# A chunk-attention and nearest-neighbour kernel: gather masks made from 256 columns, half of a comparison on ScalarE, a new order of the step, and a packed three-layer MLP

## The chip, the cores and the metric

The kernel runs on one core of a Trainium2 chip. The metric is the device time in microseconds (us) of one execution. The kernel before took 5687.46 us, the median of three runs (5677.63 to 5689.53).

A core has a matrix engine (PE, TensorE), whose weight loads are shown apart as PEld, and three engines for work by element: DVE (VectorE), ACT (ScalarE) and POOL (GpSimd). SP (SyncE) issues the DMAs here. Every engine takes its instructions in the order in which they were written; it waits where an operand is not there yet, and all that is queued behind waits with it.

## The reference

There are 32 batches. The input `x` and the context `ctx` are 32 x 128 x 1024. First comes attention in chunks of 64 positions with 8 heads, queries, keys and values all made from the context, then a residual and a normalisation over positions:

```
out = attention(ctx, ctx, ctx, mask) @ W_out.T + b_out + x
x1  = (out - mean(out)) * rsqrt(var(out) + 1e-5)
```

In the second part the context's 128 channels x 1024 positions are read again: for each of the 1024 positions the 30 nearest others (128-dimensional distance, 30 of 1024) are found. The second part takes the context as if it had three coordinates, that is, its first three rows serve as the coordinates of a point:

```
idx   = top_k(2 p.p' - |p|^2 - |p'|^2, 30)
rel   = pts[idx] - pts                      # three coordinates
sph   = (rho, theta, phi) of rel
feat  = concat(sph, sph - mean(sph))        # 6 features
h     = lrelu(bn(feat @ W1.T))              # 6 channels
h     = lrelu(bn(h @ W2.T))                 # 3 channels
h     = lrelu(bn(h @ W3.T))                 # 1 channel
att   = softmax(h over the 30 neighbours)
y     = x1 + sum over neighbours of x1[idx] * att
```

Each `bn` takes its mean and variance over all batches, points and neighbours, so each layer must have been computed for all 32 batches before the next one can be applied.

## The kernel before

The kernel has three stages, each with its own order of instructions fixed by `written_order`.

**Stage 1, the loop.** 256 steps, one per block of 128 points (8 blocks per batch). It is a software pipeline that is written out by hand in `step` (lines 899 to 947): in step `s` the engines work on block `s` (top-30), `s-1` (splitting the indices), `s-2` (one-hot masks and the gather), `s-3` (summing the gather) and `s-4` (relative coordinates). Work that happens once per batch (projections, values, normalisation, the features of a whole batch) is put into the steps by `plan` and issued by `do(s - 0.5)` and `do(s)`.

The parts that matter here, each with its lines:

- `eight` (639): three instructions of DVE (the 8 largest of 1024, their positions, their removal), four times per step, on `ds`, which ACT copies from PSUM one step ahead in `distances_copy` (631).
- `exponents` (499): DVE takes the maxima of the scores `sc`, ACT makes eight exponentials; `normalize` (512): a reciprocal on DVE, then a product on POOL.
- `split_indices` (648), `turn_indices` (655), `spread_indices` (663): the 30 indices of each point, padded to 32 slots, are written as hi = index / 8 and lo = index mod 8, turned by PE so that slots are rows, copied by ACT into `ht` (64 x 128) and written to DRAM (`hl`). SP then reads hi back as one row of 4096 columns for all 128 partitions (`hb`, 1 MB) and lo as 1024 columns (`lb`, four DMAs).
- `last_onehot` (686) and `onehot` (692): `hb` becomes a one-hot mask by comparing with the partition number. DVE does 3072 of the 4096 columns in one `is_equal`; ACT does the other 1024 as Abs and then Relu(1 - x). PE multiplies it with the coordinates (24 matmuls, `ps_g`), `evicted` (719) copies the product to `mk`.
- `lows` (713): the same pair of ACT instructions on `lb` makes lo's mask; `masked` (728): POOL multiplies `mk` with it; `summed` (735): eight matmuls into `ps_r`, which has one buffer; `found` (749) copies it on ACT, `relative` (754) subtracts on POOL.
- `turned`, `turned_copy`, `attend` (517 to 549): the probabilities are turned by PE, copied by ACT, multiplied with the values by PE, and copied by ACT into `ots`.
- `features` (764): a generator that is advanced 13 times per batch, every half step, by `turn`; its element work is on POOL, its functions on ACT.

The order of a step before, by engine: ACT has `last_onehot`, the exponentials, `split_indices`, `ht`, `distances_copy`, `turned_copy`, `lows`, `ots`, `found`, the half-step extras, `evicted`, the extras. PE has `distances`, `turn_indices`, `turned`, the 24 matmuls, `attend`, half-step extras, `scores`, `summed`, extras. DVE has the maxima, `eight` 0, `is_equal`, `eight` 1 and 2, the reciprocal, `eight` 3.

**Stage 2, the MLP** (lines 980 to 1129). The features of a batch were written to DRAM as 3 x 30720 values and come back as 120 partitions (3 channels x 40 groups) x 768 columns. The first pass computes layer 1 as four matmuls of 120 x 120 weights and 384 columns, and layer 2 as four more; the matrices hold the layer's weights in blocks, so that most entries are zero. The second pass applies layer 2's normalisation and computes layer 3; its result `zz` is written to DRAM (two DMAs, line 1102) and read back by point as `Z` (line 1103).

**Stage 3, the weighted sum** (lines 1132 to 1314). It is not touched by the change.

Of the kernel before, what the change touches and what calls it, by code (L numbers as in the profile page):

```python
# [9 lines left out]
F32 = mybir.dt.float32  # L10
U32 = mybir.dt.uint32
I32 = mybir.dt.int32
# [45 lines left out]
def kernel(ctx: ExitStack, tc: tile.TileContext, aps: dict, out: bass.AP):  # L58
# [57 lines left out]
    pi = const.tile([P, 4], I32, tag="pi", name="pi")  # L116
    nc.gpsimd.iota(pi[:, 0:1], pattern=[[0, 1]], base=0, channel_multiplier=1)
    nc.vector.tensor_scalar(pi[:, 1:2], pi[:, 0:1], 7, None, ALU.bitwise_and)
    nc.vector.tensor_scalar(pi[:, 2:3], pi[:, 0:1], 31, None, ALU.bitwise_and)
    pf = const.tile([P, 8], F32, tag="pf", name="pf")  # L120
    nc.vector.tensor_copy(pf[:, 0:3], pi[:, 0:3])
    pcol, lo_p = pf[:, 0:1], pf[:, 3:4]
    nc.vector.tensor_scalar(pf[:, 5:6], pf[:, 2:3], 24.0, None, ALU.is_lt)
    nc.vector.tensor_scalar_add(lo_p, pf[:, 1:2], 1.0)
    nc.vector.tensor_mul(lo_p, lo_p, pf[:, 5:6])
    nc.vector.tensor_scalar_add(lo_p, lo_p, -1.0)
    less_p = const.tile([P, 1], F32, tag="less_p", name="less_p")
    nc.vector.tensor_scalar_mul(less_p, pcol, -1.0)
    less_lo = const.tile([P, 1], F32, tag="less_lo", name="less_lo")
    nc.vector.tensor_scalar_mul(less_lo, lo_p, -1.0)  # L130

    own2 = const.tile([P, NJ, 2, 2], F16, tag="own2", name="own2")
    nc.vector.tensor_scalar(pi[:, 3:4], pi[:, 0:1], 3, None, ALU.logical_shift_right)
    nc.vector.tensor_copy(pf[:, 6:7], pi[:, 3:4])
    for j in range(NJ):
        for n, (col, base) in enumerate(((pf[:, 6:7], OFF + 16 * j), (pcol, 128 * j))):
            nc.vector.tensor_scalar_add(
                own2[:, j, n, :], col.to_broadcast([P, 2]), float(base)
            )
# [45 lines left out]
    def spread(name, n):  # L185
# [19 lines left out]

    NQ = 40
    NR = P * E // NQ
    CQ = 3 * NQ
    assert NR * NQ == P * E and NR % 2 == 0 and NR // 2 <= 512
    dd = const.tile([P, 3, NQ], F32, tag="dd", name="dd")  # L210
    nc.gpsimd.memset(dd, 0.0)
    nc.gpsimd.affine_select(
        out=dd, in_=dd, compare_op=ALU.not_equal, fill=1.0, base=0,
        pattern=[[-NQ, 3], [-1, NQ]], channel_multiplier=1,
    )
    own_c = const.tile([P, 3], F32, tag="own_c", name="own_c")
    nc.vector.tensor_reduce(own_c, dd, AX.X, ALU.add)
    own_q = const.tile([P, NQ], F32, tag="own_q", name="own_q")
    nc.vector.tensor_reduce(own_q, dd.rearrange("p c q -> p q c"), AX.X, ALU.add)

    def of_channel(pool, name, w, n, c=None):

        t = pool.tile([P, n, 3], F32, tag=f"{name}_3", name=f"{name}_3")
        if c is None:
            c = pool.tile([P, n], F32, tag=name, name=name)
        nc.vector.tensor_mul(t, w, own_c.unsqueeze(1).to_broadcast([P, n, 3]))
        nc.vector.tensor_reduce(c, t, AX.X, ALU.add)
        return c

    def matrix(name, w, n):  # L230

        m = const.tile([P, n, NQ], F32, tag=name, name=name)
        nc.vector.tensor_mul(
            m,
            own_q.unsqueeze(1).to_broadcast([P, n, NQ]),
            of_channel(const, f"{name}_w", w, n).unsqueeze(2).to_broadcast([P, n, NQ]),
        )
        return m.rearrange("p n q -> p (n q)")
# [14 lines left out]
    kv_h = const.tile([P, 2, 6], F32, tag="kv_h", name="kv_h")  # L253
    we_h = const.tile([P, 2, 3], F32, tag="we_h", name="we_h")
    for to, w, n in ((kv_h, kv, 6), (we_h, we, 3)):
        for h in range(2):
            of_channel(
                const, f"of_{n}_{h}", w[:, 3 * h : 3 * h + 3, :].rearrange("p c f -> p f c"), n,
                to[:, h, :],
            )  # L260
    bn1_h = [
        of_channel(const, f"bn1_h{i}", w.rearrange("p (h c) -> p h c", c=3), 2)
        for i, w in enumerate(bn_w[0])
    ]
    bn2_h = [of_channel(const, f"bn2_h{i}", w.unsqueeze(1), 1) for i, w in enumerate(bn_w[1])]

    mx1 = matrix("mx1", we, 6)
    w2s = const.tile([P, 2, 3, 3], F32, tag="w2s", name="w2s")
    nc.vector.tensor_copy(w2s, w2.rearrange("p (i h c) -> p h i c", h=2, c=3))
    mx2 = matrix("mx2", w2s.rearrange("p h i c -> p (h i) c"), 6)  # L270
# [4 lines left out]
        mx3[:, 0:NQ], own_q, of_channel(const, "mx3_w", w3.unsqueeze(1), 1), None, ALU.mult  # L275
    )
    avg_c = const.tile([P, 3, NQ], F32, tag="avg_c", name="avg_c")
    nc.vector.tensor_scalar_mul(
        avg_c, own_c.unsqueeze(2).to_broadcast([P, 3, NQ]), 1.0 / NQ
    )  # L280
    avg_c = avg_c.rearrange("p c q -> p (c q)")
# [9 lines left out]
    def root(pool, dst, v, shape, tag):  # L291
# [12 lines left out]
    sph_d = [dram.tile([3, P * E], F32, tag=f"sph_{b}", name=f"sph_{b}") for b in range(B)]  # L304
# [3 lines left out]
        [dram.tile([2 * SL, P], BF16, tag=f"hl_{b}_{j}", name=f"hl_{b}_{j}") for j in range(NJ)]  # L308
        for b in range(B)
# [8 lines left out]
    with ExitStack() as part:  # L318
# [11 lines left out]
        for j in range(NJ):  # L330
            w = p1.tile([P, 3, SL], F16, tag=f"wt{j}", name=f"wt{j}")
            nc.gpsimd.memset(w[:, 0, :], 0.0)

            nc.gpsimd.tensor_copy(w[:, 1:3, KNN:SL], own2[:, j])
            wts.append(w)
        for i in range(2):
# [6 lines left out]
            for name, rows in (("mb3", mb3s), ("nx3", nx3s)):  # L343
                m = p1.tile([P, T], BF16, tag=f"{name}{i}", name=f"{name}{i}")
                nc.gpsimd.memset(m, 0.0)
                rows.append(m)

# [150 lines left out]

# [842 lines left out]
```

## Time and profile before

The profiled execution took 5682.62 us by the clock of the runs; its span, from the first to the last instruction, is 5680.9 us.

| engine | busy us | share of the span |
|---|---|---|
| PE | 4305.4 | 76% |
| DVE | 5210.7 | 92% |
| ACT | 4105.8 | 72% |
| POOL | 2354.1 | 41% |

The stages can be told by what runs: the loop's last `is_equal` starts at 4212.0 us; the first matmul of the MLP starts at 4259.8, the last statistics of its first pass are made at 4431, those of its second pass at 4524; the first matmul of stage 3 starts at 4555.

A line of the list of groups names the source line, the engine, the operation, what is written and read, the shapes and the count, then the busy time in us and the mean length of one in ns, then how long the engine stood idle before such instructions and what ended most of that. The lines around the loop's rows:

```profile
L643 DVE MAX8 top<-ds 128x8 f32<-128x1024 f32 x1024 | 1250.5, 1221 | 10.3 <-ACT ds L634 4.6
L716 ACT ACTIVATE lb<-lb,less_lo 128x1024 bf16<-128x1024 bf16 x256 | 296.9, 1160 | 0.0
L689 ACT ACTIVATE hb<-hb,less_p 128x1024 bf16<-128x1024 bf16 x256 | 293.5, 1146 | 17.6 <-DMA hb<-hl 16.3
L717 ACT ACTIVATE lb<-lb 128x1024 bf16<-128x1024 bf16 x256 | 270.9, 1058 | 8.1
```

The first says that the 8 largest are taken 1024 times at 1221 ns, and that DVE hardly waits before them. The other three are ACT's comparisons, lo's (716, 717) and the quarter of hi's (689), each 1024 columns wide.

### The profile page before, as it was taken

Reading aid. Unit: us, or ns where it says so; the run is one execution under the profiler, and the core shown is the slowest. Engines: PE = TensorE matmul, PEld = TensorE weight load, DVE = VectorE, ACT = ScalarE, POOL = GpSimd, SP = SyncE. Lnnn points to the kernel's source line nnn. Section 1 sums busy time; section 2 is a strip of 40 time slices with the busy share of each in tenths; the row PEclk is TensorE's granted clock in tenths of the full one; section 3 lists DMA queues with packets and bytes.
Section 4 is the critical chain, followed back from the end, with each engine's and each line's share of the span. In section 5 each row is a group of like instructions: output and inputs, shape, how many; then the busy total and the mean of one; then the engine's idle time right before and its main releaser. Section 6 shows DMA issues by size and latency. Waiting matters only on the chain. (4 is left out here: it accounts for less than half of the span.)

```text
span 5680.9 us, 127216 instructions
## 1 busy us (share of the span) xinstructions
PE 4305.4 (76%) x48908; PEld 2593.5 (46%) x48908; DVE 5210.7 (92%) x6990; ACT 4105.8 (72%) x9798; POOL 2354.1 (41%) x2736
## 2 busy tenths in 40 slices
PE   6766776776677677767767776677749589999999
PEld 3433443443344334334433443334325167777776
DVE  8999999999999999999999999999975597888876
ACT  5777777777777777777777777777755576666665
POOL 3455555555655555555555555555540000000000
PEclk8878878787878888787888788788869699999999
DMA  2333333333233233333323333333322233333332
GB/s 84 108 107 105 121 112 109 108 111 111 102 116 115 102 111 116 113 110 111 111 103 110 115 107 111 111 105 117 109 92 69 72 84 98 96 97 97 95 98 84
DMA packets 318510, 589.60 MB, mean 104 GB/s; under 512 B 147408, under 2 KB 207568, under 8 KB 285136
## 3 DMA queue, kind: packets, MB, share of 16 engines
q1 hardware_dynamic: 317904, 581.47, 30.8%
q8 instruction: 387, 6.34, 0.5%
q14 instruction: 219, 1.79, 0.1%
HBM read 439.66 MB, written 74.45 MB: 90 GB/s over the span
## 5 line engine op out<-in xcount | busy, mean ns | idle before, releaser
L643 DVE MAX8 top<-ds 128x8 f32<-128x1024 f32 x1024 | 1250.5, 1221 | 10.3 <-ACT ds L634 4.6
L644 DVE FIND_INDEX8 idx<-top,ds 128x8 uint32<-128x1024 f32 x1024 | 1248.4, 1219 | 0.0
L646 DVE MATCH_REPLACE8 ds<-top,ds 128x1024 f32<-128x1024 f32 x768 | 928.8, 1209 | 0.0
L659 PE MATMUL ps_hl<-ident,wt 128*64 128x128 f16 x256 | 74.0, 289 | 1116.8 <-ACT wt L653 1116.0
L1293 PEld LDWEIGHTS <-oh 128*128 128x128 bf16 x24576 | 692.2, 96 | 333.7 <-issue 288.0
L506 ACT ACTIVATE pr<-sc,mx 128x64 f32<-128x64 f32 x2048 | 610.8, 323 | 207.7 <-DVE mx L502 138.5
L1293 PE MATMUL pss<-apart,oh 128*128 128x32 bf16 x24576 | 697.1, 176 | 41.8 <-DMA apart<-bc 34.7
L703 PE MATMUL ps_g<-hb,tp 128*32 128x512 bf16 x6144 | 651.9, 589 | 94.3 <-DVE hb L697 92.8
L758 POOL TENSOR_TENSOR rel<-got 128x90 f32<-128x90 f32 x256 | 108.3, 423 | 1359.1 <-ACT got L751 1358.9
L659 PEld LDWEIGHTS <-wt 128*64 128x64 f16 x256 | 30.7, 120 | 1306.7 <-ACT wt L653 1306.7
L733 POOL TENSOR_TENSOR mk<-mk,lb 128x512 f32<-128x512 f32 x512 | 623.5, 1238 | 1.8
L1224 DVE TENSOR_TENSOR oh<-h,ihi 128x4096 bf16<-128x4096 bf16 x256 | 584.6, 2284 | 18.6 <-PE pss L1293 18.2
L740 PEld LDWEIGHTS ps_r<-sel,mk 128*128 128x128 f32 x4096 | 511.6, 203 | 181.7 <-issue 79.2
L624 PE MATMUL pd<-cx 128*128 128x512 f32 x992 | 577.4, 666 | 0.0
L1245 PE MATMUL acc<-al,xtr 128*128 128x512 f32 x1024 | 565.5, 635 | 0.6 <-ACT al L1303 0.6
L740 PE MATMUL ps_r<-sel,mk 128*128 128x12 f32 x4096 | 535.8, 269 | 6.1 <-POOL mk L733 4.8
L1303 ACT COPY al<-pss 128x512 f32<-128x512 f32 x512 | 296.5, 585 | 223.5 <-PE pss L1293 220.3
L515 POOL TENSOR_TENSOR pr<-pr,sm 128x512 f32<-128x512 f32 x256 | 267.0, 1043 | 427.5 <-DVE sm L514 375.0
L506 ACT ACTIVATION_READ_ACCUMULATOR pr<-sc,mx 128x1 f32 x2048 | 442.5, 216 | 0.0
L703 PEld LDWEIGHTS <-tp 128*32 128x32 bf16 x6144 | 223.3, 130 | 405.3 <-issue 393.1
L1221 ACT COPY h<-hi 128x1024 bf16<-128x1024 bf16 x256 | 268.0, 1048 | 119.8 <-DVE oh L1224 119.5
L484 PE MATMUL sc<-kx,qT 128*64 128x512 f32 x1024 | 324.0, 714 | 10.4 <-DMA kx<-kT 7.3
(337 smaller groups left out, 8762.5 us busy)
## 6 DMA issues: line engine op xcount, KB each, us to landing
hb<-hl SPq DMA_DIRECT2D x256, 1024.0 KB
lb<-hl SPq DMA_DIRECT2D x1024, 64.0 KB
apart<-bc SPq DMA_DIRECT2D x1024, 48.0 KB
mb<-in_mask_Bx1x_ff_dram SPq DMA_DIRECT2D x32, 512.0 KB
xb<-in_x_dram SPq DMA_DIRECT2D x32, 512.0 KB
kx<-kT SPq DMA_DIRECT2D x512, 32.0 KB
x<-xb SPq DMA_DIRECT2D x32, 512.0 KB
xt<-xt SPq DMA_DIRECT2D x32, 512.0 KB
```

The lines of the kernel that those rows point to most:

```text
L484: nc.tensor.matmul(dst, qT[:, te : te + CHUNK], kx[:, :, te : te + CHUNK], start=True, stop=False,)
L506: nc.scalar.activation(pr_t[:, i, :], sc[:, i, :], AF.Exp, bias=mx[:, i : i + 1], accum_out=sm[:, i, :],)
L624: nc.tensor.matmul(pd, cx[:, j * P : (j + 1) * P], cx[:, sl], start=True, stop=False)
L643: nc.vector.max(top[:, sl], ds)
L644: nc.vector.max_index(idx[:, sl], top[:, sl], ds)
L646: nc.vector.match_replace(ds, top[:, sl], ds, GONE)
L703: nc.tensor.matmul(pg[e * 32 : (e + 1) * 32, :], tp[:, i, :], oh[:, e * 1024 + r * 512 : e * 1024 + (r + 1) * 512], start=(i == 0), stop=( ...
L733: nc.gpsimd.tensor_mul(half, half, lb[:, r * 512 : (r + 1) * 512])
L740: nc.tensor.matmul(pr.rearrange("p (e k) c -> p k e c", k=8)[:, k], mk[:, k, :], sel2, start=True, stop=True,)
L1224: nc.vector.tensor_tensor(oh.rearrange("p g a i -> p a g i"), h32.to_broadcast([P, 4, 32, 32]), ihi.to_broadcast([P, 4, 32, 32]), ALU.is_e ...
L1245: nc.tensor.matmul(acc.rearrange("p c g a -> p (c g) a"), xt[:, l, :], al[:, l], start=(l == 0), stop=(l == NJ - 1),)
L1293: nc.tensor.matmul(ps[:, k, :], oh[:, g].rearrange("p a i -> p (a i)"), bm[:, :, i, g, :], start=(i == 0), stop=(i == 2),)
```

## The change

1. **lo's mask.** `split_indices` writes hi and lo's source four times side by side (120 columns instead of 30). `turn_indices` makes, beside the old 64 x 128 product, two products of 128 x 128 in which every row is one pair (slot, value of lo); PE gets seven matmuls instead of two. ACT turns these 256 columns into the mask `lc` (Abs, Relu), SP writes it to DRAM (`lo`, 64 KB) and reads it back spread as `lb`, which is then a finished mask. `lows` is gone.
2. **hi's comparison.** DVE does 2048 columns, ACT 2048.
3. **A gate.** A POOL instruction of one element reads DVE's half of the mask before `masked`, so that POOL's products start after the comparison.
4. **The order of a step** as in the diff. The maxima come after `eight` 0; ACT's exponentials after the comparisons; `summed` before `scores` and `attend`; `found` before `summed`; `normalize` last. In `spread_indices` the read of `hb` is issued before the write of `nb`.
5. **`features`** is cut into 20 parts (`TURNS`), advanced every half step.
6. **The MLP** gets its data as four groups of 32 rows (30 used: 3 channels x 10 groups). Layer 1 is eight matmuls of 30 rows x 64 weight columns, layer 2 eight of 64 rows x 32 columns, in an order in which neighbours have other rows, columns and PSUM banks; `ps_h` gets three buffers. In the last layer `z` has five buffers instead of three, and the read of `Z` is issued two turns later than the write that it waits for (`by_point`).

```diff
         def turn_indices(s):
-            pt = ps_1.tile([2 * SL, P], F32, tag="ps1", name=f"ps_hl_{s}")
-            nc.tensor.matmul(pt, wt[:, SL : 3 * SL], ident1, start=True, stop=False)
-            nc.tensor.matmul(pt, wt[:, 0 : 2 * SL], ident8, start=False, stop=True)
+            hi4, all4 = flat[:, SL : 5 * SL], flat[:, 5 * SL : 9 * SL]
+            pt = ps_1.tile([P, 3, P], F32, tag="ps1", name=f"ps_hl_{s}")
+            once = pt[0 : 2 * SL, 2, :]
+            nc.tensor.matmul(once, flat[:, 4 * SL : 6 * SL], ident1, start=True, stop=False)
+            nc.tensor.matmul(once, flat[:, 0 : 2 * SL], ident8, start=False, stop=True)
+            for h in range(2):
+                nc.tensor.matmul(pt[:, h, :], all4, ident1, start=True, stop=False)
+                if h == 1:
+                    nc.tensor.matmul(pt[:, h, :], less4, ident1, start=False, stop=False)
+                nc.tensor.matmul(pt[:, h, :], hi4, ident8, start=False, stop=True)
         def spread_indices(s):
...
+            lc = p2.tile([P, 2, P], BF16, tag="lc", name=f"lc_{s}")
+            nc.scalar.activation(lc, pt[:, 0:2, :], AF.Abs, bias=from_lo)
+            nc.scalar.activation(lc, lc, AF.Relu, bias=1.0, scale=-1.0)
+            dl = lo_d[b][j]
+            nc.sync.dma_start(dl.rearrange("h x n -> x h n"), lc)
...
+            by_l = dl.rearrange("h (q e k) n -> (h q) e (k n)", q=4, e=4)
             for e in range(4):
                 nc.sync.dma_start(
                     lb[e * 32 : (e + 1) * 32, :],
+                    by_l[:, e, :].unsqueeze(0).to_broadcast([4, 8, 8 * P]),
                 )
         def last_onehot(s):
-            rest = near[s][0][:, 3 * 8 * P :]
+            rest = near[s][0][:, 2 * 8 * P :]
         def onehot(s):
-            first = oh[:, 0 : 3 * 8 * P]
+            first = oh[:, 0 : 2 * 8 * P]
...
-        def lows(s):
...
+        def gate(s):
+            passed = p2.tile([1, 1], BF16, tag="passed", name=f"passed_{s}")
+            nc.gpsimd.tensor_copy(passed, gates.pop(s)[0:1, 0:1])
         def step(s):
...
+            if past(1):
+                split_indices(s - 1)
             if past(2):
                 last_onehot(s - 2)
...
             if now:
                 eight(s, 0)
+            if now and s > 0:
+                maxima(s)
+                exponents(s)
             if past(1):
                 turned(s - 1)
             if 0 <= s and s + 1 < S:
                 distances_copy(s + 1)
             if past(2):
                 onehot(s - 2)
+                gate(s - 2)
+            if past(3):
+                masked(s - 3)
             if past(4):
                 found(s - 4)
                 relative(s - 4)
             if past(2):
                 evicted(s - 2)
             if past(3):
                 summed(s - 3)
+            if past(1):
+                turned_copy(s - 1)
             if now:
                 eight(s, 1)
...
             if s + 1 < S and s >= 0:
                 scores(s + 1)
+            if past(1):
+                attend(s - 1)
+            do(s - 0.5)
             if now:
                 eight(s, 2)
             do(s)
             if now:
                 eight(s, 3)
+                normalize(s)
```

```diff
+        TURNS = [(r, (r + w) % 2) for w in range(2) for r in range(4)]
         def first_layer(b):
...
+            for r, i in TURNS:
+                rows = slice(32 * r, 32 * r + 30)
+                nc.tensor.matmul(
+                    pss[r // 2][64 * (r % 2) : 64 * (r % 2) + 64, i, 0:half],
+                    mx1[rows], x[rows, i * half : (i + 1) * half], start=True, stop=True,
+                )
         def second_layer(b):
...
+            for r, i in TURNS:
+                rows = slice(64 * (r % 2), 64 * (r % 2) + 64)
+                nc.tensor.matmul(
+                    ps[32 * r : 32 * r + 32, i, 0:half],
+                    mx2[rows], hs[r // 2][rows, i * half : (i + 1) * half],
+                    start=True, stop=True,
+                )
         def third_layer(b):
...
-            z = q2.tile([P, half], F32, tag="z", name=f"zz_{b}", bufs=3)
+            z = q2.tile([P, half], F32, tag="z", name=f"zz_{b}", bufs=5)
...
+        def by_point(b):
             nc.sync.dma_start(Z[:, b, :], z_d[b].rearrange("(p e) -> p e", e=E))
```

The features are written by four DMAs per batch instead of one, and one more DMA per batch (`clear`) fills the unused rows with zeros.

## The prediction, made before the changed kernel was run

> **What bounds the kernel now.** I read the busy time by stretch first, over a piece of the loop and over the two passes of the MLP (columns: us; busy us and count of PE, PEld, DVE, ACT, POOL; granted clock; DMA share; GB/s).
>
> ```profile
> 1000.00:4000.00 3000.00, 2131.78 (x16266) 1197.29 (x16264) 2951.95 (x4112) 2318.33 (x6255) 1702.78 (x1953) 0.81 0.32 110
> ```
> ```profile
> 4259.00:4431.00 172.00, 167.89 (x514) 94.63 (x514) 93.52 (x145) 90.55 (x98) 0.00 (x0) 0.99 0.20 59
> 4437.00:4524.00 87.00, 46.27 (x128) 9.44 (x128) 46.32 (x69) 44.78 (x64) 0.00 (x0) 0.54 0.27 82
> ```
>
> DVE is busy 2952 of 3000 us in the loop: it is the bound, and the list of waits has no entry for it there. The maxima (line 502) start first at 34.9 and last at 4183.0 us, so 255 steps take 16.27 us each. The first MLP pass is PE's (168 of 172 us). In the second no engine is busy for more than 54%: something is waited for.
>
> For what ACT does in its idle 682 us I read its waits over the same 3000 us, some 184 steps or 23 batches (us, times, longest), and SP's:
>
> ```profile
> ACT qT L459 <- PE ps_q L458: 119.4, 46, 3.4
> ACT f_ay L822 <- POOL f_ay L821: 95.5, 23, 4.3
> ACT pr L506 <- DVE mx L502: 87.1, 63, 3.2
> ACT ht L667 <- PE ps_hl L660: 87.1, 184, 0.6
> ACT ots L547 <- PE ps_ot L540: 71.9, 115, 1.4
> ```
> ```profile
> SPq L669 <- ACT ht L667: 1771.8, 184, 14.9
> ```
>
> Only 87 us of it, with 51 us behind POOL before the same exponentials, is ACT waiting for the slower loop. ACT works 12.57 us per step and waits 3.70; without those 138 us and 6 us of DMA its own chain, waits on PE included, is 15.5 us per step against DVE's 16.27. **That is the thin margin on which this change turns.** SP has 9.6 us per step to spare.
>
> **DVE's part.** Its comparison shrinks from 3072 to 2048 columns.
>
> ```profile
> L697 DVE TENSOR_SCALAR hb<-hb,pf x256: 1008/1012/1871, 65.0 to 4212.0; 128x3072 bf16<-128x3072 bf16 x128
> ```
>
> Minimum, median and maximum: half of them take 1.01 us, the others are stretched while POOL runs its product with lo's mask beside them (mean 1.204). The gate keeps that product away, so I start from 1.01. A third less in proportion gives 0.67; with some 0.2 us fixed (the reciprocal of 8 columns takes 0.194) it is 0.74. I take 0.74: 1.204 - 0.74 = 0.46 us, and DVE could step in **15.81 us**. What the gate delays: POOL stands before `masked`, `relative`, the extras and the product in `normalize`, for which PE's `summed` and `turned` wait. POOL works 1703 / 184 = 9.2 us per step, so about 4 us lost between the last product and the comparison fit; in the step with `features` parts 15 and 16 and the splits POOL ends late, but PE's next gather waits for ACT's masks anyway. Without that cover 0.2 to 1 us in one step of eight.
>
> **ACT's part, per step.** ACT's length grows by (1.900 - 1.048) / 1024 = 0.83 ns per column, from the 2048-column cast of line 1195 and the 1024-column copy of line 1221.
> - hi: 1024 columns more in two instructions: +1.70.
> - `lows` gone: 1160 + 1058 ns less about 0.06 of overlap: -2.16.
> - `lc`, 256 columns: 0.364 (ht, 128 columns from PSUM) + 0.11, then 1.058 - 0.64, less overlap: +0.83.
> - the split's 90 more columns in two instructions: +0.15.
>
> Sum +0.52: 13.09 us of work. The waits count as much. PE's seven small matmuls (0.1 to 0.3 each) lie under the 3.9 us of `last_onehot` that now come before `ht`, so the 0.47 us wait for `ht` goes. But `ots` becomes late. `ps_r` has one buffer; PE may start `summed` only when ACT's `found` has emptied it, and the new order puts `scores` and `attend` behind `summed`. One step of PE before:
>
> ```profile
> 2542.93 0.40 PE L540 MATMUL ps_ot<-pts,vx 128*32 128x64 f32 x16
> 2543.27 1.08 PE L484 MATMUL sc<-kx,qT 128*64 128x512 f32 x4
> 2544.18 0.39 PE L488 MATMUL sc<-mb,ones 128*64 128x512 bf16 x2
> 2544.49 1.96 PE L740 MATMUL ps_r<-sel,mk 128*128 128x12 f32 x16
> 2546.38 1.04 PE L375 MATMUL ps_c<-ident,cx 3*128 3x3 f32 x8
> ```
>
> Start to start: attend 0.34, scores 1.22, summed 1.89; in the steps around it up to 0.58, 1.96 and 1.81. With the middle of these PE needs 1.8 + 1.5 + 0.5 + 0.1 = 3.9 us, begun 0.33 us after `found` starts. ACT meanwhile has `found`, `evicted` and `turned_copy`, 1.6 us from start to start (0.12 + 0.95 + 0.47, and a handover). It waits **2.6 us** where it waited 0.39. The extras come straight behind `attend` on PE now: per batch I count waits of 1.75 (sum of squares, 1.95 us of matmuls), 1.45 (transposition and values), 1.15 and 0 (projections), 0.9 (output product and squares), together 5.25 us instead of 15.8, mostly because the query projection no longer stands behind `summed` (-119 us) and the arctangent no longer waits for POOL (-95).
>
> ACT's chain: 13.09 + 2.6 + 5.25 / 8 = **16.35 us**. It is later than DVE's 15.81, and so it sets the step: 16.35 - 16.27 = +0.08, less some slack in light steps; I put +0.06 x 255 = **+15 us**. Ends: DVE alone, -0.46 x 255 = -117; and ACT with PE's slow rows throughout (below).
>
> **SP** gets one write and a wait for it ahead of `lb`. The write is issued behind `hb`, 1 MB that took 6.5 us (issued 2019.26, ACT released 2025.78), so SP stands some 6.5 us. Queued behind are `lb`, the eight `kx` copies (5.40 us of issue in one step), loads, and the next step's index write, which must put `hb` in place. Its 9.6 us of spare become about 2.6. Taken as hidden: it removes nothing, so no gain, and it costs up to 1 us in two steps of eight (+64) if the reserve is gone. Loop tail and constants: 0, within 5.
>
> **The MLP's first pass.** A batch before:
>
> ```profile
> 4312.07 2.74 PE L1049 MATMUL ps_h<-F,mx 120*120 120x384 f32 x8
> 4314.65 2.74 PE L1049 MATMUL ps_l<-h,mx 120*120 120x384 f32 x8
> 4317.23 2.74 PE L1049 MATMUL ps_h<-F,mx 120*120 120x384 f32 x8
> ```
>
> 5.16 us for eight products, 0.645 each. Now there are sixteen, 10.3 us if one follows another. The trace shows no row groups abreast. The nearest rows: two f32 products on 64 columns each take 0.91 us (line 484) where one on 128 takes 0.86 (line 624), so 1.9 of 2 run abreast; bf16 on 32 columns, 24 in 2.32 us (0.097 each against 0.22 for line 627), 2.3 of 4. [...]
>
> **The second pass.** The period settles at 2.75 us:
>
> ```profile
> 4458.48 0.34 SPq L1103 DMA_DIRECT2D Z<-z  x1
> 4458.52 0.48 ACT L1098 COPY zz<-ps_z 128x384 f32<-128x384 f32 x1 [1.14 <-DMA z<-zz]
> 4458.87 0.73 SPq L1102 DMA_DIRECT2D z<-zz  x2
> 4461.26 0.34 SPq L1103 DMA_DIRECT2D Z<-z  x1
> ```
>
> SP waits for the write's landing before it issues the read, and with it the next write; ACT waits for the buffer. The first batches, with buffers free, step in about 1.4 us. With the read two turns later SP needs 1.07 us and ACT 1.03 + 0.48: 1.5 us. The pass took 86 us; 34 x 1.5 + 1.5 = 52: **-34 us** (ends -37 and -20).
>
> **Sum**: +15 - 47 - 34 = -66 us on 5682.6, 5617; on the median of 5687.5, **5621**, said as 5620.
>
> **Rivals.**
> - *DVE stays the bound* (20%). For it: ACT's handovers are sums of small terms, and the old chain did hide. Against: 2.6 us before `ots` in every step. -117 - 47 - 34 = -198: 5490.
> - *PE's chain behind `found` holds ACT longer* (23%), the slower side. If every step has the slow rows (1.96 + 0.62 + 1.83), the wait is 3.3 instead of 2.6: 17.0 us, +185 us; 5790. It decides from a step of 16.59 us, where the 81 us of the MLP are used up. For it: half of the rows seen are slow, and SP's thin reserve adds to it; against: the pause before `summed` is new.
> - *Row groups do not run abreast* (6%): +165 instead of -47: 5833.
> - The likeliest, ACT taking over at about the old step, 47%, holds 5550 to 5700; 4% for what I don't see.
>
> Range 5480 to 5760: it takes in DVE's case and half of the slower one; about a fifth lies outside. 0.2% is 11 us. Faster: all of DVE's 20, about 40 of the likeliest, 2: 0.62. Same: 0.05. Slower: 0.33.
>
> **What would show it.** Step right if: the comparison lasts about 0.74 us with hardly a stretch; maxima 16.3 us apart while DVE is idle some 3% of the loop, waiting for `ds`; `ots` waiting for PE about 2.6 us in nearly all steps; `summed` released by ACT's `got`; a first pass of about 125 us and a second of about 52. A loop at 15.8 us with DVE never waiting, or `ots` waiting well over 3 us, would overturn the middle; a first pass over 172 us the MLP part.

## The result: 9 per cent slower, all of it in the loop

The changed kernel takes 6199.39 us, the median of four runs (6189.49 to 6213.02); the kernel before, run beside it, 5688.49. The ratio is 1.0904, with an interval of 1.0875 to 1.0932. The forecast was 5620, and the range ended at 5760.

The profiled execution has a span of 6187.8 us against 5680.9, +507. The maxima (now line 520) start first at 35.6 and last at 4793.7 us: **18.66 us per step** instead of 16.27, and so +610 us over 255 steps. The two passes of the MLP, from first matmul or activation to last statistics, take 104.1 and 45.4 us instead of 171.6 and 86.0, -108. The rest is within 6 us.

### The loop's profile after

The busy time over the same stretch as before, then the two longest entries of ACT's waits over the whole run (us, times, longest):

```profile
1000.00:4000.00 3000.00, 2239.84 (x14733) 1269.93 (x14890) 2540.46 (x3571) 2081.34 (x5415) 1450.56 (x1854) 0.75 0.31 99
```
```profile
ACT ots L569 <- PE ps_ot L562: 1171.5, 256, 5.4
ACT al L1361 <- PE pss L1351: 241.8, 244, 2.8
```

The stretch holds 159 steps. ACT works 2081 / 159 = 13.09 us in each, as was forecast, and before `ots` it waits 1171.5 / 256 = 4.58 us in every one, not 2.6. With 1.0 us before the extras that is the whole step: 13.09 + 4.58 + 1.0 = 18.7. No engine is busy for more than 85 per cent, and DVE, at 2540 of 3000 us, is no longer the bound: ACT waits for PE while, at another time of the step, PE waits for ACT. One step of PE (start, length, what it was idle for before):

```profile
2509.14 1.47 PE L740 MATMUL ps_g<-hb,tp 128*32 128x512 bf16 x22 [1.55 <-ACT hb L726]
2513.76 1.93 PE L776 MATMUL ps_r<-sel,mk 128*128 128x12 f32 x16 [3.15 <-ACT got L787]
2515.61 1.71 PE L503 MATMUL sc<-kx,qT 128*64 128x512 f32 x4
2517.09 0.65 PE L507 MATMUL sc<-mb,ones 128*64 128x512 bf16 x2
2517.68 0.65 PE L562 MATMUL ps_ot<-pts,vx 128*32 128x64 f32 x16
```

PE finishes the gather, pauses 3.15 us for ACT's copy `got` (`found`), and then does `summed`, `scores` and `attend` in one run. Over the 3000 us it waits so in 152 of the 159 steps (us, times, longest):

```profile
PE ps_r L776 <- ACT got L787: 422.1, 152, 3.3
```

The time of the step above in windows of 1 us; the number after POOL's is the granted clock, as a share of full speed:

```profile
2511.00:2512.00 1.00, 0.00 (x0) 0.00 (x0) 0.96 (x2) 1.00 (x9) 0.00 (x0) 1.00 0.00 0
2512.00:2513.00 1.00, 0.00 (x0) 0.00 (x0) 1.00 (x1) 1.00 (x6) 0.00 (x0) 1.00 0.96 213
2514.00:2515.00 1.00, 1.00 (x12) 1.00 (x11) 1.00 (x3) 1.00 (x3) 0.08 (x1) 1.00 1.00 401
2515.00:2516.00 1.00, 1.00 (x9) 0.79 (x10) 0.97 (x3) 0.07 (x1) 0.00 (x0) 0.97 0.62 139
2516.00:2517.00 1.00, 1.00 (x4) 0.20 (x2) 0.96 (x2) 0.00 (x0) 0.00 (x0) 0.50 0.00 0
2517.00:2518.00 1.00, 1.00 (x16) 0.32 (x16) 1.00 (x2) 0.00 (x0) 0.00 (x0) 0.50 0.07 23
2518.00:2519.00 1.00, 1.00 (x15) 0.59 (x6) 1.00 (x3) 0.60 (x3) 0.07 (x1) 0.50 0.20 64
2519.00:2520.00 1.00, 1.00 (x3) 0.42 (x2) 1.00 (x2) 0.97 (x3) 0.83 (x3) 0.83 0.24 90
```

PE's column shows the pause (0.00 busy), and 2 us behind it the clock falls to 0.50 for some 3.4 us. What runs then is what ACT, idle from 2515.1 to 2518.4, waits for. In most steps the half clock comes earlier and takes `summed` too (all of it in 70 of the 159 steps, a part in 61): half of its products last 367 ns or more, where the median before was 259. With `scores` it is plainer still. Its two f32 products take 1.08 us where the clock is full from end to end and 1.98 where it is half. Over the same 3000 us they ran wholly at half clock in 11 of 184 steps before, and in 132 of 159 now. The products of `summed` before (ns; minimum, median, maximum):

```profile
L740 PE MATMUL ps_r<-sel,mk x2929: 259/259/390, 1011.5 to 4000.0; 128*128 128x12 f32 x196
```

Read from the timeline between 1500 and 2500 us, 54 steps: from `found` to `summed` 0.45 us, from there to `scores` 2.91, to `attend` 2.27, to `ots` 0.72, 6.35 us in all, where the forecast had 4.2.

### The comparison and the MLP after

```profile
L733 DVE TENSOR_SCALAR hb<-hb,pf x256: 742/745/1633, 63.1 to 4821.3; 128x2048 bf16<-128x2048 bf16 x128
```

Minimum and median are 742 and 745 ns (forecast 0.74 us), but the 256 take 223.9 us, 0.875 in the mean. The gate keeps the product with lo's mask away: before, it lay beside 62 of the 93 comparisons that took over 1.05 us, now beside none of the 256. The other 31 lay beside other work of POOL, 30 of them beside the residual's products (`ys`, `xb`). Now 76 take over 0.8 us, all beside other work of POOL: `normalize` (33 of them), the residual (28) and the features (28) above all.

Of the MLP's passes first the busy time, then some of PE's rows:

```profile
4879.00:4981.00 102.00, 97.94 (x1016) 34.83 (x1008) 89.72 (x136) 83.39 (x98) 0.00 (x0) 0.95 0.33 102
4987.00:5034.00 47.00, 29.27 (x128) 7.03 (x128) 44.36 (x68) 42.24 (x64) 0.00 (x0) 0.93 0.52 160
```
```profile
4922.03 1.63 PE L1127 MATMUL ps_l<-h,mx 64*32 64x384 f32 x16
4923.59 1.52 PE L1112 MATMUL ps_h<-F,mx 30*64 30x384 f32 x16
4925.04 1.49 PE L1127 MATMUL ps_l<-h,mx 64*32 64x384 f32 x16
```

A row is one layer of a batch, and two follow each other in 1.45 + 1.56 = 3.0 us. The sixteen products of the two, at the 0.645 us that a product of the old shape took, would need 10.3. By that estimate they run 3.4 abreast; how long one of the new shape takes with no other beside it, no run shows. In the second pass the chain behind the write is gone:

```profile
5005.71 0.34 SPq L1159 DMA_DIRECT2D Z<-z  x1
5006.10 0.75 SPq L1156 DMA_DIRECT2D z<-zz  x2
5006.78 0.52 ACT L1152 COPY zz<-ps_z 128x384 f32<-128x384 f32 x1
5006.94 0.34 SPq L1159 DMA_DIRECT2D Z<-z  x1
```

The period is 1.3 us (2.75 before), and DVE is busy 44 of 47 us.

### The profile page after: what moved, and what is told of

Read it like the earlier page. It is cut to its first block, busy times and chain, and to the rows that moved or that the text cites. A ratio compares the mean times of both kernels' runs of the same rounds, so it can differ in the third digit from the quotient of the medians.

```text
span 6187.8 us, 131621 instructions
## 1 busy us (share of the span) xinstructions
PE 4828.6 (78%) x50446; PEld 2893.2 (47%) x50700; DVE 5171.5 (84%) x6991; ACT 4207.2 (68%) x9798; POOL 2323.0 (38%) x3002
## 4 chain that ended last, share of the span: by engine, by line
PE 45%; ACT 33%; issue 9%; DVE 8%; DMA 2%; SPq 2%; POOL 1%; ACTq 0%; DVEq 0%; POOLq 0%
PE ps_r L776 12%; ACT pr L528 9%; PE pss L1351 8%; PE sc L503 7%; PE acc L1303 7%; ACT hb L725 7%; ACT ds L656 4%; PE ps_ot L562 2%; DVE idx L666 2%; DVE top L665 2%; PE sc L507 2%; DVE ds L668 2%; PE ps_n L403 2%; ACT lc L705 1%; ACT ht L698 1%
## 5 line engine op out<-in xcount | busy, mean ns | idle before, releaser
L776 PE MATMUL ps_r<-sel,mk 128*128 128x12 f32 x4096 | 769.9, 330 | 676.4 <-ACT got L787 673.4
L776 PEld LDWEIGHTS ps_r<-sel,mk 128*128 128x128 f32 x4096 | 751.7, 283 | 824.1 <-issue 820.6
L569 ACT ACTIVATE ots<-ps_ot,cols 128x128 f32<-128x128 f32 x256 | 94.0, 367 | 1171.5 <-PE ps_ot L562 1171.5
L740 PE MATMUL ps_g<-hb,tp 128*32 128x512 bf16 x6144 | 543.8, 446 | 273.6 <-ACT hb L726 266.5
L646 PE MATMUL pd<-cx 128*128 128x512 f32 x992 | 641.7, 734 | 25.5 <-issue 16.2
L769 POOL TENSOR_TENSOR mk<-mk,lb 128x512 f32<-128x512 f32 x512 | 580.5, 1151 | 2.5 <-issue 0.3
L725 ACT ACTIVATE hb<-hb,less_p 128x2048 bf16<-128x2048 bf16 x256 | 509.2, 1989 | 0.0
L503 PE MATMUL sc<-kx,qT 128*64 128x512 f32 x1024 | 492.9, 1061 | 15.5 <-ACT pr L528 8.2
L726 ACT ACTIVATE hb<-hb 128x2048 bf16<-128x2048 bf16 x256 | 489.0, 1910 | 8.1
L520 DVE TENSOR_REDUCE mx<-sc 128x8 f32<-128x512 f32 x256 | 176.7, 690 | 363.0 <-PE sc L507 362.6
```

What stands on the lines that cost most here:

```text
L503: nc.tensor.matmul(dst, qT[:, te : te + CHUNK], kx[:, :, te : te + CHUNK], start=True, stop=False,)
L646: nc.tensor.matmul(pd, cx[:, j * P : (j + 1) * P], cx[:, sl], start=True, stop=False)
L725: nc.scalar.activation(rest, rest, AF.Abs, bias=less_p)
L740: nc.tensor.matmul(pg[e * 32 : (e + 1) * 32, :], tp[:, i, :], oh[:, e * 1024 + r * 512 : e * 1024 + (r + 1) * 512], start=(i == 0), stop=( ...
L776: nc.tensor.matmul(pr.rearrange("p (e k) c -> p k e c", k=8)[:, k], mk[:, k, :], sel2, start=True, stop=True,)
```

## The experiments

A step is the time from the first to the last start of the maxima, over 255; the wait is ACT's before `ots`, per step; the clock is the mean over the span. Ratios are to the kernel before, run on the same chip (5688 to 5707 us there), with 95 per cent intervals.

| kernel | us | ratio | step | wait | clock |
|---|---|---|---|---|---|
| before | 5688 | 1 | 16.27 | 0.38 | 0.841 |
| changed | 6199 | 1.090 [1.088, 1.093] | 18.66 | 4.58 | 0.797 |
| `summed` last | 6023 | 1.057 [1.055, 1.060] | 17.96 | 0.74 | 0.791 |
| `found` first | 5490 | 0.964 [0.961, 0.966] | 15.91 | 1.65 | 0.839 |
| old order, new masks | 5879 | 1.032 [1.030, 1.034] | 17.39 | 1.28 | 0.835 |
| before + MLP | 5584 | 0.980 [0.978, 0.982] | 16.26 | 0.40 | 0.841 |
| changed, pause filled | 5718 | 1.002 [1.001, 1.003] | 16.72 | 3.00 | 0.909 |
| changed, 3072 to 1024 | 5826 | 1.021 [1.018, 1.024] | 17.17 | 4.50 | 0.801 |
| `summed` last, filled | 5511 | 0.965 [0.963, 0.968] | 16.07 | 0.68 | 0.892 |
| `found` first, no gate | 5558 | 0.973 [0.970, 0.976] | 16.17 | 1.73 | 0.839 |

### 1. Where the time is: four parts

**`summed` last.** PE's order alone:

```diff
-            if past(3):
-                summed(s - 3)
             if past(1):
                 turned_copy(s - 1)
...
             if past(1):
                 attend(s - 1)
+            if past(3):
+                summed(s - 3)
             do(s - 0.5)
```

> The changed kernel with one edit: on PE the eight products of `summed` stand behind `scores` and `attend` again, ahead of the extras; ACT's, DVE's, POOL's and SP's orders are as changed. T1 (the loop is slow because `scores` and `attend` stand behind `summed`, which stands behind ACT's `found`, so ACT waits 4.6 us per step before `ots`): that wait falls below 1 us, some 1 us of it comes back as waits of the extras, the step falls from 18.66 to 16.0 to 16.5 us, the time from 6199 to 5560 to 5680 us. T2 (ACT's own added work, the half of hi's comparison, sets the step): ACT's 13.1 us stay, the step stays above 18 us, over 6050 us. T3 (the masks come late by SP's longer way of lo): over 6100 us, the waits move to another line.

Measured: 6022.53 us. The wait before `ots` fell below 1 us as T1 said, but the step only to 17.96. ACT's waits show where it went:

```profile
ACT qT L478 <- PE ps_q L477: 177.2, 41, 5.0
ACT nf L408 <- PE ps_n L403: 136.9, 21, 6.5
ACT ots L569 <- PE ps_ot L562: 123.6, 165, 0.8
ACT ys L577 <- PE ps_y L575: 95.5, 41, 3.8
```

Nearly all came back before the extras. T1 as put, that two groups of products stand in the wrong place, **fell**; 6022 us is also less than T2 and T3 allowed. PE now pauses ahead of `scores`, for the exponentials (1.95 us), and ahead of `attend` (1.26), the clock is as low as in the changed kernel, and the median product of `summed` is still 367 ns.

**`found` first.**

```diff
+            if past(4):
+                found(s - 4)
+                relative(s - 4)
             if past(1):
                 split_indices(s - 1)
...
-            if past(4):
-                found(s - 4)
-                relative(s - 4)
             if past(2):
                 evicted(s - 2)
```

> The changed kernel with one edit: `found` and `relative` stand at the head of the step, ahead of the splits and the comparison, so that the one buffer of `ps_r` is long empty when PE reaches `summed`; PE's own order is as changed. T1: PE goes from the gather straight to `summed`, without the pause of 3.3 us, so `ots` waits under 1.5 us: a step of 16.0 to 16.8 us, 5560 to 5760 us, and a higher granted clock. If it is PE's order by itself (three groups of products ahead of `ots`, whatever releases them) that makes ACT wait: above 5950 us. T2 and T3: over 6050 us.

Measured: 5490.45 us, below every kernel so far and below T1's range; `ots` waits 1.65 us, a little over T1's 1.5. `ps_r` is empty when PE comes to it, so `summed` follows the gather directly, as in this step (PE's rows):

```profile
2518.24 1.48 PE L740 MATMUL ps_g<-hb,tp 128*32 128x512 bf16 x24
2519.65 1.96 PE L776 MATMUL ps_r<-sel,mk 128*128 128x12 f32 x16
2521.53 1.08 PE L503 MATMUL sc<-kx,qT 128*64 128x512 f32 x4
```

PE's order is the changed one and ACT's work too, so neither by itself is the cause; the wait for `found` inside that order is.

```profile
1000.00:4000.00 3000.00, 2427.83 (x17624) 1364.54 (x17616) 2945.41 (x4208) 2457.77 (x6412) 1725.55 (x2178) 0.80 0.37 117
```

DVE is the bound again, 2945 of 3000 us. The clock of the loop, 0.80, is no higher than the 0.81 of the kernel before: what counts here is which products run at half clock, and who waits for them. The median product of `summed` takes 259 ns, as before, where the changed kernel has 367.

**Old order, new masks.** The changed kernel with the step of the kernel before (its `exponents` is `maxima` and `exponents` now), but for this place:

```diff
-            if past(3):
-                masked(s - 3)
...
             if past(2):
-                lows(s - 2)
                 onehot(s - 2)
+                gate(s - 2)
+            if past(3):
+                masked(s - 3)
```

> The changed kernel (lo's mask from 256 columns, half of hi's comparison on ACT, the gate, 20 parts of features, the packed MLP) with the order of a step of the kernel before; only `masked` stands behind the gate. T1 (the order is the cause): ACT's work of 13.1 us with the old waits of some 3 us per step gives 16.0 to 16.4 us, 5530 to 5640 us. T2 (the work moved to ACT is the cause): over 6000 us. T3 (SP's way of lo): over 6000 us.

Measured: 5879.16 us, a miss of every theory. ACT's waits over 172 steps:

```profile
ACT ots L569 <- PE ps_ot L562: 221.6, 172, 1.4
ACT ht L698 <- PE ps_hl L690: 192.5, 172, 1.2
ACT qT L478 <- PE ps_q L477: 93.7, 43, 2.9
```

`ht` now waits 1.12 us per step for the seven small products (0.47 before for two), and `ots` 1.29 (0.39 before): `lows`, 2.2 us of ACT's work, had stood between `turned_copy` and `ots` and covered PE's `attend`. By these waits the new masks do need another order than the old one; no run tests these two waits apart.

**The MLP alone.** The kernel before with the second diff of the change (and what belongs to it: `clear`, four DMAs of the features, the padded constants, three buffers of `ps_h`).

> The kernel before with the MLP of the changed one alone: four row groups, the padded features, three buffers of `ps_h`, five of `z`, the read of `Z` two turns later; the loop is as before but for three more DMAs per batch for the features and one for the zeros. All theories agree that the MLP gains: by the changed kernel's trace the first pass takes 101 us instead of 172 and the second 47 instead of 87, so 5575 us (5560 to 5595). If the DMAs of the features or the zeros disturb the loop: above 5600 us.

Measured: 5584.31 us, its step 16.26. The MLP gives 116 us by the medians, and its DMAs cost the loop nothing.

### 2. The clock

**The changed kernel with the pause filled.** More work for PE, and nothing else:

```diff
+        def fill(s):
+            pt = spare.pop(s)
+            for i in range(10):
+                nc.tensor.matmul(pt[:, 3, :], ident, ident, start=True, stop=True)
...
+            if past(1):
+                fill(s - 1)
             if past(3):
                 summed(s - 3)
```

> The changed kernel with ten more f32 matmuls of 128 x 128 per step (some 2.5 us of PE, into unused columns of `ps_hl`, read by nobody) between the gather and `summed`, where PE pauses 3.15 us for `found`. Theory C (in the windows of 1 us of the changed kernel the granted clock reads 1.00 in the pause and then 0.50 for some 3.3 us, just when `summed`, `scores` and `attend` run; so it is the pause that makes these slow): the granted clock rises from 0.797 to 0.85 or more, the products of `summed` go from a median of 367 ns back to 259, the wait of `ots` falls from 4.6 to 2.6 to 3.2 us, and the time falls by 300 to 450 us to 5750 to 5900, although PE does more work. Theory D (the rows are slow for another reason, or the clock falls with load): clock 0.80 or lower, rows as slow, 6200 us or more.

Measured: 5718.12 us, **481 us less for 2560 useless products**. The clock of the span is 0.909, higher than in the kernel before. The busy time, the wait and the products of `summed` (line 782 here; ns, minimum, median, maximum), with the row of the changed kernel in a fence of its own:

```profile
1000.00:4000.00 3000.00, 2489.77 (x20041) 1562.48 (x20219) 2831.63 (x3989) 2324.41 (x6057) 1661.69 (x2085) 0.89 0.35 111
```
```profile
ACT ots L569 <- PE ps_ot L562: 769.1, 256, 5.7
```
```profile
L782 PE MATMUL ps_r<-sel,mk x2859: 178/259/368, 999.7 to 3998.6; 128*128 128x12 f32 x191
```
```profile
L776 PE MATMUL ps_r<-sel,mk x2544: 251/367/370, 1011.1 to 3986.4; 128*128 128x12 f32 x196
```

The median is back from 367 to 259 ns, the wait at 769.1 / 256 = 3.00 us, the step at 16.72. In windows of 1 us from 2513 to 2530 us the clock reads 1.00 throughout. Theory C holds (the gain is somewhat over its 300 to 450 us), theory D falls. Of the 2.39 us that the changed kernel lost per step, 1.94 go with the clock; as the clock with filler is above that of the kernel before, this is what a clock kept up is worth, not the exact price of the fall.

**`summed` last, filled**: eight such products at the other pause.

```diff
+            if past(1):
+                fill(s - 1)
             if s + 1 < S and s >= 0:
                 scores(s + 1)
```

> The kernel in which `summed` stands behind `scores` and `attend` (6022 us), with eight matmuls of 128 x 128 in f32 per step, read by nobody, ahead of `scores`, where PE pauses 1.9 us for the exponentials. Theory C: the pause halved the clock here too (median of the products of `summed` 367 ns), and ACT's waits before the extras, some 3.5 us per step, came from the slow products; filled, the clock is over 0.85, the median 259 ns, the time 5650 to 5850 us. Theory D or a wait that only moves: 6000 us or more.

Measured: 5510.97 us, 512 us less than without them and below the 5650 that was expected at the least; clock 0.892, median of `summed` 260 ns. A good part of the miss of `summed` last is explained by this: ACT's four longest waits before the extras (`qT`, `nf`, `ys`, `nx`) fall from 491 us of the 3000, 2.9 per step, to 333, 1.8 per step, once the products are no longer slow.

**The split back**, 3 for 2 in `last_onehot` and `onehot`:

```diff
-            rest = near[s][0][:, 2 * 8 * P :]
+            rest = near[s][0][:, 3 * 8 * P :]
...
-            first = oh[:, 0 : 2 * 8 * P]
+            first = oh[:, 0 : 3 * 8 * P]
```

> The changed kernel with hi's comparison split 3072 to 1024 again; order, gate, lo's mask and MLP as changed. ACT loses 1.70 us of work ahead of `found`, DVE gets some 0.37 us more. If ACT's work counts one for one in the step and nothing else follows: 18.66 - 1.70 = 16.96 us, 5765 us. Theory C in addition: PE's pause before `summed` shrinks from 3.15 to some 1.5 us, the clock stays up and the wait of `ots` falls too: DVE's 16.2 us become the bound, 5570 to 5680 us. If the work on ACT has no part in it: 6150 us or more.

Measured: 5825.52 us. The step loses 1.49 of the 1.70 us, but the wait (4.50 us) and the clock (0.801) stay, and the shorter pause that theory C had added here did not come: PE waits 411.7 us for `got` in 144 steps, 2.86 us in the mean, and 422.1 in 152, 2.78 us, in the changed kernel. The half comparison stretches the ring by its own length and does not make the pause: it stands ahead of the gather too, so gather and `found` both come earlier. The pause is what stands on ACT between the masks and `found`: `ht`, `lc`, the exponentials and `ds`.

### 3. The gate

```diff
             if past(2):
                 onehot(s - 2)
-                gate(s - 2)
```

> The kernel that has `found` first (5490 us) without the gate. There DVE is the bound again (2945 of 3000 us busy), so what the gate does for the comparison counts: if POOL's product stretches it as in the kernel before (1.20 us against 1.01, a fifth), 0.745 us become some 0.89, 0.15 us per step, 5530 us. If the gate's wait costs more than it saves: below 5480 us.

Measured: 5557.96 us, 68 us more than with it (52 by the ratios, as the two ran on different chips). First the comparison without the gate, then with it:

```profile
L733 DVE TENSOR_SCALAR hb<-hb,pf x256: 701/1028/3239, 62.2 to 4182.3; 128x2048 bf16<-128x2048 bf16 x128
```
```profile
L733 DVE TENSOR_SCALAR hb<-hb,pf x256: 701/745/1798, 61.1 to 4114.5; 128x2048 bf16<-128x2048 bf16 x128
```

Without it the median is 1.03 us instead of 0.75, and the step is 16.17 us instead of 15.91; 0.26 x 255 is 66 us: the gate pays, by more than the 0.15 us per step that was expected.

### 4. More from the best order

Two runs filled PE's pauses in the kernel with `found` first, the second with more of hi on ACT.

```diff
+            if past(1):
+                fill(s - 1)
             if past(1):
                 turned(s - 1)
```
```diff
-            rest = near[s][0][:, 2 * 8 * P :]
+            rest = near[s][0][:, 12 * P :]
...
-            first = oh[:, 0 : 2 * 8 * P]
+            first = oh[:, 0 : 12 * P]
```

> The kernel that has `found` first (5490 us), with six such matmuls per step ahead of `turned`, where PE still pauses at times for POOL's product or the masks. DVE is the bound there, so theory C gives little: clock from 0.84 to 0.90, the wait of `ots` from 1.6 to about 1 us, 5460 to 5500 us. If the added work holds the gather up: above 5520 us.

> As the last, with hi's comparison split 1536 to 2560: DVE loses some 0.18 us per step, ACT gets 0.85 us. If the filled pauses leave ACT that much room: 5430 to 5470 us. If ACT is the bound as soon as DVE is not: ACT's chain of 15.9 us grows by 0.2 to 0.8 us, 5540 to 5690 us.

Measured: 5763.65 and 6077.00 us, both far off. PE's longest waits in the first:

```profile
PE ps_hl L697 <- ACT lc L711: 589.1, 176, 3.8
PE ps_hl L685 <- ACT wt L675: 66.5, 44, 2.2
```

The added products (line 697) write the tile `ps_hl` while ACT has yet to read `lc` from it: 589.1 / 176 = 3.3 us per step of a new wait. Their clock rose to 0.899 and 0.875 all the same, so they don't show what it is worth here. Two more put the products into the empty bank of `ps_r`, behind `turned` (the second with 14 in place of 12 in the split above):

```diff
+        def fill(s):
+            room[s] = ps_1.tile([P, 256], F32, tag="psr", name=f"ps_r_{s}", bufs=1)
+            for i in range(4):
+                nc.tensor.matmul(
+                    room[s][:, P : 2 * P], ident, ident, start=True, stop=True
+                )
...
+            if past(3):
+                fill(s - 3)
             if past(2):
                 onehot(s - 2)
```

> The kernel that has `found` first (5490 us) with four matmuls of 128 x 128 in f32 per step, read by nobody, between `turned` and the gather; they go to the bank of `ps_r`, which is empty there, and not to `ps_hl`, whose reading by ACT made PE wait 3.3 us per step in the run before. If theory C holds here: clock from 0.84 to 0.88 or more, the wait of `ots` from 1.6 to about 1.0 us; DVE, busy 98 per cent, lets the time fall by 20 to 60 us only: 5430 to 5470 us. If the matmuls (1 us) are in the gather's way: 5500 to 5650 us.

> As the last, with hi's comparison split 1792 to 2304: DVE has 0.09 us less per step, ACT 0.42 us more. If the clock leaves ACT room: 5420 to 5460 us. If ACT sets the step beside DVE: 5500 to 5570 us.

Measured: 5466.10 us (0.960, interval 0.959 to 0.962) with clock 0.889, step 15.83 and wait 1.28 us; and **5445.69 us (0.957, interval 0.956 to 0.959)**, step 15.75, the fastest version found. DVE is busy 2946 of 3000 us in both. The interval of the first touches that of `found` first (0.961 to 0.966), so the filler alone gains little where DVE is the bound.

### 5. The new order with the old masks

To see whether the order alone costs, the kernel before got it, with `lows` between `found` and `ots`, without gate and MLP:

```diff
             if past(1):
                 turned_copy(s - 1)
+            if past(2):
+                lows(s - 2)
```

In a first run the pair of `lows` worked on `mk` in place of `lb`, so lo's mask wasn't made and the product was altered.

> The kernel before with the new order of a step alone (no gate; `lows` stands behind `turned_copy`, that is, between `found` and `ots`; 13 parts of features, old masks, old MLP). If the order alone makes the loop slow: over 6050 us. If it is the order together with what the new masks put ahead of `found` and take away behind it: ACT's front is 1.7 us of comparison and 0.9 us of `lc` shorter, so PE hardly pauses, and the 2.2 us of `lows` lie under the wait of `ots`: a step of 15.9 to 16.6 us, 5600 to 5770 us.

> The order of a step alone once more, with `lows` on the tile `lb` (in the run before it was on `mk`). If the order alone makes the loop slow, because `found` holds `summed` and `normalize` stands last whatever the masks: a step over 17.2 us, 5930 us or more. If it takes the new masks too: 15.9 to 16.6 us, 5600 to 5770 us.

Measured: 6003.88 and 6000.21 us (both 1.052), a step of 17.4: the order alone does cost. PE's waits in the second:

```profile
PE ps_pt L521 <- POOL pr L515: 348.7, 63, 10.5
PE ps_r L740 <- ACT got L751: 235.1, 116, 2.4
```

The first, up to 10.5 us, is for POOL's product of `normalize`. Four runs then took the parts apart: `found` first (the edit shown above); `normalize` back behind the third `eight`; both; and `found` first, `normalize` last, with the features in 20 parts as in the change. The second's edit:

```diff
             if now:
                 eight(s, 2)
+                normalize(s)
             do(s)
             if now:
                 eight(s, 3)
-                normalize(s)
```

> The order of a step alone (6000 us: old masks, old MLP) with `found` and `relative` at the head of the step. If PE's pause for `found` and the half clock behind it are what the order costs: the step falls from 17.4 to 16.0 to 16.6 us, 5620 to 5780 us. If it is `normalize` at the end of the step (PE waits 2.1 us per step for POOL's product before `turned`): over 5900 us.

> The order of a step alone (6000 us) with `normalize` behind the third `eight` again, as before the change. If `normalize` at the end is what the order costs: 5620 to 5780 us. If it is `found`: over 5900 us.

> The new order with old masks, with `found` first and `normalize` behind the third `eight` (the two together; singly they took 117 and 92 us from the 6000). If the two are all that the order costs: 5680 to 5800 us. If they only add and something else stays, such as POOL's long parts of `features` ahead of the products that PE waits for: 5800 us or more.

> The new order with old masks, `found` first, `normalize` last, and `features` in 20 parts instead of 13. PE's longest wait for POOL's product of `normalize` was 10.5 us, in the steps with long parts. If these long parts are what makes `normalize` last dear: 5650 to 5780 us. If not: 5850 us or more.

Measured: 5883.41, 5908.01, 5872.43 and 5686.53 us. Neither `found` nor `normalize` explains it, singly (117 and 92 us) or together (128). With both moved, PE hardly waits for the product of `normalize` any more (up to 1.8 us), but it waits up to 6.8 us for POOL's other product, `mk`:

```profile
PE ps_r L740 <- POOL mk L733: 235.9, 44, 6.8
```

Cut into 20 parts, the features take 197 us more away than `found` first alone, and PE's longest wait for the product of `normalize` falls to 4.6 us. So the waits point to the length of the features' parts on POOL. The cut moves some of ACT's work on the features too, and no run adds the 20 parts alone to the first of these kernels, so how the gain divides stays open. With `found` first and 20 parts the order costs nothing (0.997, interval 0.996 to 0.998; step 16.26), though the clock of the span is lower than before, 0.809 against 0.841. The changed kernel has the 20 parts, so this cost is not what made it slow.

## Why the prediction was wrong, point by point

- **ACT's work** (13.09 us) was right. The mechanism was right too: `summed` held by `found`, `scores` and `attend` behind it, ACT late at `ots`.
- **The comparison** was right as a median only. The sum 1.204 - 0.74 sets out from a mean, and the mean fell to 0.875: DVE saved 0.33 us, not 0.46, as other work of POOL still stretched it. In the changed kernel DVE isn't the bound, so this isn't what failed.
- **The step that failed** is the term "it waits **2.6 us** where it waited 0.39": it measured 4.58. It came from 1.8 + 1.5 + 0.5 + 0.1 us for PE's chain, "with the middle" of rows of the kernel before. I took the spread of these rows (1.22 to 1.96 from start to start for `scores`) as a scatter to be averaged; it was two clocks (1.08 and 1.98 us for its f32 products). The chain measured 2.91 + 2.27 + 0.72 because it stands behind a pause that the change itself makes (3.15 us in the step shown).
- **The slower rival** had the rows at the slow end, and against it I put "the pause before `summed` is new". That was the wrong way round: the pause is the reason for the slow rows. And that rival was too mild: its 1.83 us for `summed` is a row at full clock. In the kernel before no step between 1000 and 4000 us had `summed` wholly at half clock; in the changed kernel it then takes 3.56 us.
- With the clock kept up by filler the step is 16.72 us and the wait 3.0 us, near the forecast's 16.33 and 2.6. So the sum for an undisturbed PE was short by 0.4 us, and the other 1.94 us are the clock.
- The trace has the clock at 1.00 or 0.50 only, and in the step shown at 0.50 behind a pause of 3.15 us, which stands behind one of 1.55. I did not look at the pause, whose length (`ht`, `lc`, the exponentials and the copy of `ds` against a gather of 1.5 to 2.4 us) could have been added up from the rows.
- **The rival "DVE stays the bound"**, 5490 us, is what the order with `found` first gives: 5490.45. That the figures meet is luck: 92 us less come from the loop by its steps, where I had 117, and 116 from the MLP, where I had 81. The 92 fit the comparison's mean there, 0.857 us over the 63 of 1500 to 2500 us: (1.204 - 0.857) x 256 = 89 us.
- **SP hidden** was right: in the changed kernel SP still waits 1141.5 us of 3000 for `lc`.
- **The MLP** gained 68 and 41 us; forecast 47 and 34. No run shows the time per batch that the 47 of the first pass stood for; the runs show 3.0 us per batch where it was 5.16, so that by the estimate above the products ran 3.4 abreast. The kernel before with the MLP alone confirms the sum.

## What to carry to other kernels

Before a group of matmuls is moved behind a wait, add up how long PE will stand idle there: here the price was the pause (3.15 us) and a lower clock (0.50 for some 3.4 us) for what came after it, and that landed on whoever waited for PE (ACT, 4.58 us per step). Where rows of one operation differ by a factor of up to two (here 1.08 and 1.98 us), read the granted clock in short windows beside them before taking a mean. The cure is an earlier release (here one copy moved to the head of the step, 709 us less) or, where there is none, work to fill the pause (481 us less), written where nobody still reads (where ACT still read, PE waited 3.3 us per step).

## What the runs showed of the hardware that was not expected

Useless matmuls made a kernel 8 per cent faster, and another as well (6199 to 5718, 6023 to 5511 us).

Two short pauses went with as low a clock here as one long one, and the half clock outlasted them by far. In the kernel with `summed` last, whose loop has a clock of 0.74 (0.75 in the changed kernel), PE pauses 1.95 us before 2514.59 and 1.26 before 2517.15, and in windows of 1 us the clock reads:

```profile
2515.00:2516.00 1.00, 0.89 (x6) 0.12 (x2) 0.47 (x1) 1.00 (x5) 0.28 (x1) 0.90 0.96 360
2516.00:2517.00 1.00, 0.00 (x0) 0.00 (x0) 0.96 (x3) 1.00 (x3) 0.10 (x1) 0.50 0.96 377
2519.00:2520.00 1.00, 1.00 (x6) 1.00 (x6) 1.00 (x3) 0.99 (x2) 0.00 (x0) 0.50 0.00 0
2525.00:2526.00 1.00, 1.00 (x2) 0.15 (x1) 0.97 (x3) 1.00 (x1) 1.00 (x2) 0.50 0.16 35
2526.00:2527.00 1.00, 1.00 (x10) 0.46 (x9) 1.00 (x1) 0.91 (x1) 1.00 (x1) 0.98 0.03 4
```

It is 0.50 for some 10.2 us, although PE is busy without a break from 2517.15 to 2529 us. In the step of the changed kernel it was 3.41 us. Between 1000 and 4000 us the trace of the kernel before records 196 stretches at 0.50: 74 of 3.41 us, 100 of 6.83 and 22 of 10.24; the changed kernel has 183, of 3.41 to 20.5 us. The time at full clock, cut into pieces of 3.41 us, can be sorted by how long PE was busy in each, and by the clock of the 3.41 us that followed:

| PE busy in the piece | before: pieces, half clock followed | changed: pieces, half clock followed |
|---|---|---|
| under 40 per cent | 166, 166 | 113, 113 |
| 40 to 70 | 50, 0 | 188, 66 |
| over 70 | 321, 29 | 135, 4 |

So little work in a piece went with half clock behind it in both kernels, but half clock came behind busier pieces too. Nor did work alone end it at once, as the 10.2 us show. Why was not found out.
